# Layer 3 of a graph network: x0 times all three weights ahead of its first product, with nodes on partitions and x0's own term parked in DRAM

## The chip, the cores and the metric

The kernel runs on one core of a Trainium2 chip, in one launch. The metric is the device time in microseconds of one execution. TensorE (PE) multiplies into PSUM, VectorE (DVE) and ScalarE (ACT) move and combine results, GpSimd (POOL) and SyncE (SP) here mostly issue DMAs. All data are float32; in the trace each float32 matmul shows as two records, a transpose as one.

## The reference, cut to what matters

Four layers act on x, of 8 batches, 2048 nodes and 64 features. `A` is one 2048 x 2048 adjacency matrix, normalised by rows. Every layer ends with `x = layernorm(x + layer(x))`. The last two, the ones concerned here, are:

```python
# layer 2
out = x @ W_self + (A @ x) @ W_neigh + bias
# layer 3: support0 and support1 are both A
x1 = A @ x0;  x2 = 2 * A @ x1 - x0        # once for each support
out = concat([x0, x1, x2, x1, x2]) @ weight + bias
```

With equal supports layer 3 is three terms: `x0 (W0 - W2 - W4) + A x0 (W1 + W3) + A (A x0) (2 (W2 + W4))`, then the bias. It needs two products with A in any order of factors: `A (A x0 W_AA + x0 W_A) + x0 W_X + b`.

## The kernel before, in words

**Storage.** `xy` holds two copies of the activations in SBUF ("slots" 0 and 1), nodes on partitions: 16 tiles of 128 nodes, 512 columns (8 batches of 64 features). A "group" g is 512 nodes (4 tiles), a "pair" p is 128 columns (two batches); `part(g, p, slot)` is one 128 x 512 piece. A quarter is 1024 nodes by 256 columns, so four parts.

**A product.** `product(src, feature, ...)` computes A times slot `src` by two levels of a Strassen scheme: seven outer products A11, S1, A12, S2, S4, S3, A22, in that order, each of seven inner ones in `inner`. That makes 49 block products a product, each of a 512 x 512 piece of A (or a sum of pieces, kept in DRAM as `comb`) with a 512 x 128 operand. `load` fetches the 1 MB piece over SP's queue into a ring of 4 + 3 buffers. A block product has one of two forms:

- without `onto_slot` (line 277): four matmuls, x stationary, 512 columns of A moving. The result has features on partitions, and a "feature" function multiplies it with a weight.
- with `onto_slot` (line 270): sixteen matmuls, A stationary, 128 columns of x moving. The result has nodes on partitions, and DVE adds it straight onto the slot.

DVE forms the operand sums (t1 to t4, T) and joins the partial results (u2, u3, C); ACT copies the first partial result (p1, line 295). Three PSUM banks hold the block products and are reused by every inner product.

**Other work among the blocks.** After every block product `pump.step(rate)` lets queued generators run some steps (`jobs` first in order; `later` holds deferred ones that wake by a count of steps). So the projections, transposes and layernorms of finished parts stand between the block products in PE's instruction order. A tile framework sets the final order on each engine and the waits; it is static.

**Layers 2 and 3**, in the order of the program:

1. layer 2, `product(0, then(nothing, 1), onto_slot=1)`: slot 1 += A times slot 0, then layernorm (two pairs at a time, lines 505 to 533), which leaves x0 of layer 3 in slot 1.
2. layer 3, `product(1, feature3, own=both_terms(1, w3o, b3), rate=1.5)`: A x0 with features on partitions. For every result part `feature3` does four matmuls with W_AA (`project`, line 1161), and DVE adds them to slot 0 (line 1213). Beside it `both_terms` transposes each pair of x0 (line 1152, copied by ACT at line 1154), multiplies it with two weights (line 1190: 64 rows by 128 columns, the two batches of a pair on the two halves of the rows), and ACT and DVE bring the two results to slots 0 and 1 (lines 1195 and 1196).
3. layer 3, `product(0, then(nothing, 1, single=[(1, 0)], store=True), rate=2, onto_slot=1, ends=True)`: slot 1 += A times slot 0, layernorm, store.

PSUM beside the three banks of the products: one pool `p_z` of five banks for transposes and projections. The weights lie in `wd` (block diagonal) and `w3o`, summed and centered once early (`sum_weights`, lines 611 to 630).

Of the kernel before, what the change touches and what calls it, by code (L numbers as in the profile page):

```python
# [9 lines left out]
F32 = mybir.dt.float32  # L10
AF = mybir.ActivationFunctionType
ALU = mybir.AluOpType
AX = mybir.AxisListType
PSUM = bass.MemoryType.PSUM
DRAM = bass.MemoryType.DRAM

P = 128
EPS = 1e-5
GW = 512
TG = GW // P  # L20
# [84 lines left out]
def kernel(  # L105
# [18 lines left out]
    nc = tc.nc  # L124
# [3 lines left out]
    F = b_l0.shape[1]  # L128
    B = BF // F
    NT = N // P  # L130
    NG = N // GW
    NP = B // 2
# [5 lines left out]
    const = ctx.enter_context(tc.tile_pool(name="const", bufs=1))  # L138
# [4 lines left out]
    dram = ctx.enter_context(tc.tile_pool(name="dram", bufs=1, space=DRAM))  # L143
# [4 lines left out]
    xy = big.tile([P, 2, NT, BF], F32, tag="xy", name="xy")  # L148
# [26 lines left out]
    ident = const.tile([P, P], F32, tag="ident", name="ident")  # L175
    make_identity(nc, ident)

    W1A, W1B, W2N, W2S, W3X, W3A, W3AA = range(7)
    wd = const.tile([P, 7, P], F32, tag="wd", name="wd")

    w3o = const.tile([P, 2, F], F32, tag="w3o", name="w3o")
    w2o = const.tile([P, 2, F], F32, tag="w2o", name="w2o")
    b2 = const.tile([P, F], F32, tag="b2", name="b2")
    b3 = const.tile([P, F], F32, tag="b3", name="b3")

# [3 lines left out]
    def part(g, p, slot):  # L189
        return xy[:, slot, g * TG : (g + 1) * TG, ts(p, 2 * F)]  # L190
# [277 lines left out]
    def tiles_of(i):  # L468
        return slice(i * TG, (i + 1) * TG)

    class Norm:
# [18 lines left out]
        def center(self):  # L490
            sm = self.new("sm")
            nc.vector.tensor_reduce(sm, self.v, AX.X, ALU.add)
            nc.vector.scalar_tensor_tensor(self.v, self.wide(sm), -1.0 / F, self.v, ALU.mult, ALU.add)
# [54 lines left out]
    def layernorm(i, p0, n, slot, mean=False, store=False, pool_sq=False):  # L548

        norm = Norm(tiles_of(i), p0, n, slot, str(n), pin=False)  # L550
        if mean:
            norm.center()
        norm.square(pool_sq)
        yield
        norm.add_up()
        norm.variance()
        norm.root()
        norm.refine()
        norm.scale()
        if store:  # L560
            norm.store()
        yield

    def then(feature, slot, single=(), gap=0, after=None, **kw):


        seen = set()

        def both(i, p, hT):
            yield from feature(i, p, hT)  # L570
            seen.add((i, p))
            if (i // 2, p // 2) in single:
                yield from layernorm(i, p, 1, slot, **kw)
            elif (i, p ^ 1) in seen:
                norm = layernorm(i, p - p % 2, 2, slot, **kw)
                if gap:
                    pump.defer(norm, gap, need=i < NG // 2)
                else:
                    yield from norm
                if after is not None:  # L580
                    pump.defer(after(i, p - p % 2), 6, 2, i < NG // 2)
        return both


    if True:
# [8 lines left out]
        def load_weights():  # L594
            nc.gpsimd.memset(wd, 0.0)
            w3 = sums.tile([P, 5, F], F32, tag="t", name="w3", bufs=5)
            for k in range(2):
                half = slice(k * F, (k + 1) * F)
                for i, src in ((W1A, w_l1[0]), (W1B, w_l1[1]), (W2N, w_neigh), (W2S, w_self)):
                    nc.sync.dma_start(wd[half, i, half], src)  # L600
                nc.scalar.dma_start(w3[half], w_l3.rearrange("(k i) o -> i k o", i=F))
            nc.sync.dma_start(b2, b_l2.to_broadcast([P, F]))
            nc.sync.dma_start(b3, b_l3.to_broadcast([P, F]))
            return w3

        def sum_weights(w3):
            pin = tc.keep_in_program_order

            for k in range(2):
                half = slice(k * F, (k + 1) * F)  # L610
                pin(nc.vector.tensor_tensor(wd[half, W3A, half], w3[half, 1], w3[half, 3], ALU.add))
                pin(nc.vector.tensor_tensor(w3[half, 2], w3[half, 2], w3[half, 4], ALU.add))
                pin(nc.vector.tensor_tensor(wd[half, W3X, half], w3[half, 0], w3[half, 2], ALU.subtract))
                pin(nc.vector.tensor_scalar(wd[half, W3AA, half], w3[half, 2], 2.0, None, ALU.mult))


            for k in range(2):
                half = slice(k * F, (k + 1) * F)
                center(wd[half, W2N:, half], half, pin=pin)
            for w in (W2S, W3X):  # L620
                pin(nc.vector.tensor_tensor(wd[:, w, :], wd[:, w, :], ident, ALU.add))
            for k in range(2):
                half = slice(k * F, (k + 1) * F)
                for n, w in enumerate((W3A, W3X)):
                    pin(nc.vector.tensor_copy(w3o[half, n], wd[half, w, half]))
                for n, w in enumerate((W2N, W2S)):
                    pin(nc.vector.tensor_copy(w2o[half, n], wd[half, w, half]))
            center(b2.unsqueeze(1), pin=pin)
            center(b3.unsqueeze(1), pin=pin)

# [83 lines left out]
        with tc.tile_pool(name="p_n", bufs=4, space=PSUM) as p_n, tc.tile_pool(  # L714
            name="p_tn", bufs=2, space=PSUM
        ) as p_tn, tc.tile_pool(name="p_b", bufs=1, space=PSUM) as p_b, tc.tile_pool(
            name="xs", bufs=1
# [271 lines left out]
            for ns in range(TG):  # L989
                ch = [chunks.pop((ns, j)) for j in range(NG)]  # L990
                if ns == 0:
# [15 lines left out]
                    hT = next(first4)  # L1007
                    next(parts)
                    w3 = load_weights()
                    load_chunks(1, *AHEAD)  # L1010
                    pump.add(biases())
                else:
                    hT = fast_slice(ns, ch, held, parts if ns == 1 else ())
# [121 lines left out]
            product(1, then(feature0, 0, gap=4, pool_sq=True), lambda: pump.add(sum_wn()), rate=4, runs=RUNS)  # L1135


    late = p_z = None

    def to_late():  # L1140
        nonlocal late, p_z, p_mm2, ring2, loads
        first.close()
        late = ctx.enter_context(tc.tile_pool(name="late", bufs=1))
        ring2 = ctx.enter_context(tc.tile_pool(name="ring2", bufs=3))
        loads = 0
        p_mm2 = ctx.enter_context(tc.tile_pool(name="p_mm2", bufs=1, space=PSUM))
        p_z = ctx.enter_context(tc.tile_pool(name="p_z", bufs=5, space=PSUM))

    def pair_transposed(g, p, slot):
        pt = p_z.tile([P, GW], F32, tag="z", name="pt2")  # L1150
        for k in range(TG):
            nc.tensor.transpose(pt[:, ts(k, P)], xy[:, slot, g * TG + k, ts(p, 2 * F)], ident)  # L1152
        xT = late.tile([P, GW], F32, tag="xT", name="xT", bufs=2)
        nc.scalar.copy(xT, pt)
        return xT

    def project(terms):
        z = p_z.tile([P, TG, P], F32, tag="z", name="z")
        for k in range(TG):
            for n, (aT, w) in enumerate(terms):  # L1160
                nc.tensor.matmul(  # L1161
                    z[:, k, :], aT[:, ts(k, P)], wd[:, w, :],
                    start=(n == 0), stop=(n == len(terms) - 1),
                )
        return z
# [6 lines left out]
    def feature1b(g, p, hT):  # L1172
        z = project([(hT, W1B)])
        nc.vector.scalar_tensor_tensor(part(g, p, 0), z, 0.0, part(g, p, 0), ALU.max, ALU.add)
        yield

    product(0, feature1a, to_late, pin=True)
    def both_terms(src, w, b):

        def own(g, p):  # L1180

            xTs = [pair_transposed(g, p + q, src) for q in range(2)]
            yield

            zs = [[p_z.tile([P, TG, 2, F], F32, tag="z", name="z2") for _ in range(2)] for _ in range(2)]
            for z, xT in zip(zs, xTs):
                for k in range(TG):
                    for n in range(2):
                        half = slice(n * F, (n + 1) * F)
                        nc.tensor.matmul(z[n][:, k], xT[half, ts(k, P)], w[half], start=True, stop=True)  # L1190
            tiles = slice(g * TG, (g + 1) * TG)
            for q, z in enumerate(zs):
                for n in range(2):
                    cols = ts(2 * (p + q) + n, F)
                    nc.scalar.copy(xy[:, 0, tiles, cols], z[n][:, :, 0])
                    nc.vector.tensor_tensor(
                        xy[:, 1, tiles, cols], z[n][:, :, 1],
                        b.unsqueeze(1).to_broadcast([P, TG, F]), ALU.add,
                    )
            yield  # L1200
        return own

    def nothing(g, p, c):

        yield from ()


    product(1, then(feature1b, 0, mean=True, after=both_terms(0, w2o, b2)), rate=2)
    product(0, then(nothing, 1), onto_slot=1)


    def feature3(g, p, hT):
        nc.vector.tensor_tensor(part(g, p, 0), project([(hT, W3AA)]), part(g, p, 0), ALU.add)
        yield

    product(1, feature3, own=both_terms(1, w3o, b3), rate=1.5)
    product(0, then(nothing, 1, single=[(1, 0)], store=True), rate=2, onto_slot=1, ends=True)
    pump.drain()


# [45 lines left out]
```

## Time and profile before

| what | us |
|---|---|
| median of 3 runs | 1666.83 (1666.49 to 1666.88) |
| the profiled execution | 1666.76 |
| its span | 1665.0 |
| layer 2, second product, from the start of the span | 1092.17 to 1276.44 |
| layer 3, first product | 1276.44 to 1482.44 |
| layer 3, second product with its tail | 1482.44 to 1665.00 |

The profile is of one execution. Its time is 1.76 us longer than its span, and 0.07 us from the median. The clock granted to PE was full throughout (0.999). Busy shares are shares of the span. In the timeline the columns are start, length, engine, line, operation, output and inputs, shape, count of records; a bracket names the idle time before and what ended it. [...] the distance between starts is the cost, not the length.

### The profile page before, as it was taken

What the parts mean: (1) busy time and instruction counts of PE and PEld (TensorE: products, weight loads), DVE (VectorE), ACT (ScalarE), POOL (GpSimd) and SP (SyncE); (2) the same over time, 40 slices, a digit from 0 to 9 for tenths busy, and PEclk for the clock granted to TensorE, in tenths of its full rate; (3) what the DMA queues carried; (4) which work ended last, traced back from release to release, by engine and by line L of the source; (5) the groups of instructions that cost most, each with busy time, mean ns of one, the idle gap of its engine ahead of it and who ended that gap; (6) DMA issues with size and microseconds to landing.
All of it is one profiled execution on the core that took longest, in us unless ns stands there. A gap on an engine that the chain in (4) does not pass through costs nothing.

```text
span 1665.0 us, 21271 instructions
## 1 busy us (share of the span) xinstructions
PE 1656.7 (100%) x8414; PEld 1060.6 (64%) x8414; DVE 965.9 (58%) x1737; ACT 276.0 (17%) x810; POOL 246.1 (15%) x332
## 2 busy tenths in 40 slices
PE   9999999999999999999999999999999999999998
PEld 5988844444444444444454455599998455579998
DVE  5986895656456456655434365873668344453657
ACT  0200110242142144430010011220001011100001
POOL 1221200254155056550000000000000000000000
PEclk9999999999999999999999999999999999999999
DMA  8998899504503600019877867657888866678884
GB/s 318 340 383 310 316 322 326 200 26 162 205 26 129 250 26 26 26 65 364 290 266 278 304 254 257 229 218 272 291 297 299 306 209 233 230 264 294 316 311 167
DMA packets 81074, 391.56 MB, mean 235 GB/s; under 512 B 8944, under 2 KB 25584, under 8 KB 41040
## 3 DMA queue, kind: packets, MB, share of 16 engines
q1 hardware_dynamic: 68288, 346.78, 58.2%
q0 software_dynamic: 11248, 42.08, 6.7%
q10 hardware_dynamic: 1440, 1.35, 0.3%
q8 instruction: 67, 1.10, 0.3%
q14 instruction: 31, 0.25, 0.0%
HBM read 339.85 MB, written 50.33 MB: 234 GB/s over the span
## 4 chain that ended last, share of the span: by engine, by line
PE 95%; DVE 3%; DMA 1%; issue 0%; SPq 0%; DVEq 0%
PE y L1109 20%; PE mmb L277 17%; PE mma L277 12%; PE mmc L277 12%; PE mmb L270 9%; PE ps_n L918 7%; PE mma L270 6%; PE mmc L270 6%; PE z L1161 3%; PE z L1190 2%; PE ps_i L832 1%; DVE si L640 1%; DMA xy<-in_x 1%; PE pt L1152 1%; DMA bias<-in_b_l 0%; DVE so L640 0%
## 5 line engine op out<-in xcount | busy, mean ns | idle before, releaser
L277 PE MATMUL mmb<-a,t 128*128 128x512 f32 x648 | 292.0, 593 | 0.0
L1119 DVE SCALAR_TENSOR_TENSOR xy<-y,e_sb,xy 128x128 f32<-128x128 f32 x512 | 179.6, 351 | 141.2 <-PE y L1109 125.3
L277 PEld LDWEIGHTS mmb<-a,t 128*128 128x128 f32 x648 | 121.5, 190 | 145.3 <-issue 143.5
L1128 POOL TENSOR_TENSOR s<-s 128x512 f32<-128x512 f32 (+2 forms) x192 | 157.4, 820 | 333.0 <-ACT s L1123 322.8
L1123 ACT ACTIVATE s<-y,e_sb 128x128 f32<-128x128 f32 x512 | 139.3, 383 | 231.5 <-PE y L1109 231.5
L228 DVE TENSOR_TENSOR u<-mmb,p 128x512 f32<-128x512 f32 x84 | 57.9, 689 | 176.5 <-PE mmb L277 121.1
L270 PE MATMUL mmb<-t,a 128*128 128x128 f32 x1344 | 156.9, 275 | 0.0
L270 PEld LDWEIGHTS mmb<-t,a 128*128 128x128 f32 x1344 | 153.5, 192 | 0.0
L1109 PE MATMUL y<-wn,xT 64*128 64x512 f32 x512 | 131.5, 590 | 0.0
L1109 PE MATMUL y<-wn,C 64*128 64x512 f32 x512 | 131.2, 589 | 0.0
L1109 PE MATMUL y<-wn,tT 64*128 64x512 f32 x512 | 131.2, 589 | 0.0
L277 PE MATMUL mma<-a,T 128*128 128x512 f32 x256 | 115.5, 594 | 0.0
L277 PE MATMUL mmc<-a,t 128*128 128x512 f32 x216 | 97.3, 592 | 0.0
L295 ACT COPY p<-mma 128x512 f32<-128x512 f32 x42 | 24.7, 588 | 405.8 <-PE mma L277 248.4
L1109 PEld LDWEIGHTS y<-wn,xT 64*128 64x128 f32 x512 | 49.3, 187 | 61.2 <-issue 60.7
L1109 PEld LDWEIGHTS y<-wn,tT 64*128 64x128 f32 x512 | 49.6, 187 | 60.2 <-issue 60.2
L1109 PEld LDWEIGHTS y<-wn,C 64*128 64x128 f32 x512 | 49.5, 187 | 60.3 <-issue 60.3
L277 PE MATMUL mma<-a,xy 128*128 128x512 f32 x192 | 86.6, 594 | 0.3 <-PE pt_n L465 0.3
L277 PEld LDWEIGHTS mma<-a,T 128*128 128x128 f32 x256 | 47.6, 190 | 56.8 <-issue 56.5
L228 DVE TENSOR_TENSOR C<-mmc,C 128x512 f32<-128x512 f32 x48 | 33.2, 692 | 85.9 <-PE mmc L277 75.1
L277 PEld LDWEIGHTS mmc<-a,t 128*128 128x128 f32 x216 | 40.0, 190 | 45.4 <-issue 45.2
L277 PEld LDWEIGHTS mma<-a,xy 128*128 128x128 f32 x192 | 36.0, 190 | 44.4 <-issue 43.8
(160 smaller groups left out, 2127.5 us busy)
## 6 DMA issues: line engine op xcount, KB each, us to landing
a<-comb SPq DMA_DIRECT2D x240, 1024.0 KB, 4.8
a<-in_blocks SPq DMA_DIRECT2D x54, 1024.0 KB, 4.8
comb<-si POOLq DMA_DIRECT2D x28, 1024.0 KB, 6.2
a<-in_slices SPq DMA_DIRECT2D x15, 1024.0 KB, 9.0
comb<-so POOLq DMA_DIRECT2D x15, 512.0 KB, 9.6
t1T<-hT SPq DMA_DIRECT2D x16, 256.0 KB, 4.6
xT<-in_xT SPq DMA_DIRECT2D x16, 256.0 KB, 3.0
tT<-t1T SPq DMA_DIRECT2D x16, 256.0 KB, 3.1
```

Source lines behind the costliest of these rows:

```text
L228: nc.vector.tensor_tensor(out, a, b, op)
L270: nc.tensor.matmul(to, a[:, k, m, :], xb[:, m, :], start=(start and opens and m == 0), stop=(m == TG - 1), skip_group_check=True,)
L277: nc.tensor.matmul(ps, xb[:, m, :], a[:, :, m, :], start=(start and m == 0), stop=(m == TG - 1), skip_group_check=True,)
L295: nc.scalar.copy(p1, pa)
L640: tc.keep_in_program_order(nc.vector.tensor_tensor(out, a, b, op))
L918: nc.tensor.matmul(ps[:, ts(p, GW // 2)], b(k, p), a(k // TG, k % TG), start=(start and p == k == 0), stop=(k == NT // 2 - 1), skip_group_ ...
L1109: mm = nc.tensor.matmul(y[:, b, :], terms[n][half, ts(k, P)], wn[half, n, h * DH : (h + 1) * DH, :], start=(n == 0), stop=(n == 2),)
L1119: nc.vector.scalar_tensor_tensor(acc, y[:, :, ts(d, F)], e, acc, ALU.mult, ALU.add)
L1123: nc.scalar.activation(s[:, d], y[:, :, ts(d, F)], AF.Copy, scale=e)
L1128: nc.gpsimd.tensor_tensor(s[:, :n], s[:, :n], s[:, n : 2 * n], ALU.add)
L1161: nc.tensor.matmul(z[:, k, :], aT[:, ts(k, P)], wd[:, w, :], start=(n == 0), stop=(n == len(terms) - 1),)
L1190: nc.tensor.matmul(z[n][:, k], xT[half, ts(k, P)], w[half], start=True, stop=True)
```

## The change

Layer 3's weights are applied before the first product instead of after it. When layer 2's second product has finished and normalised two pairs, the new `three_terms` transposes x0 as before and multiplies each pair with all three weights at once (64 rows by 192 columns). Two results go by ACT into slots 0 and 1 (x0 W_AA and x0 W_A); the third, x0 W_X plus the bias, is made by DVE in `rest` and stored to DRAM (`x3`) by POOL's queue. The first product of layer 3 then runs with nodes on partitions, straight onto slot 1; meanwhile `rest_of` loads `x3` back into slot 0 where it is no longer read. The second product adds onto slot 0. `feature3` and its `project` calls are gone; `wd` shrinks to two weights.

```diff
-    product(0, then(nothing, 1), onto_slot=1)
+    product(0, then(nothing, 1, after=three_terms), to_wide, rate=1.5, onto_slot=1)
...
-    def feature3(g, p, hT):
-        nc.vector.tensor_tensor(part(g, p, 0), project([(hT, W3AA)]), part(g, p, 0), ALU.add)
+    def rest_of(g, p):
+        for q in range(2):
+            nc.gpsimd.dma_start(part(g, p + q, 0), x3[g, p + q].rearrange("p (t c) -> p t c", t=TG))
         yield
...
-    product(1, feature3, own=both_terms(1, w3o, b3), rate=1.5)
-    product(0, then(nothing, 1, single=[(1, 0)], store=True), rate=2, onto_slot=1, ends=True)
+    product(0, nothing, own=rest_of, onto_slot=1)
+    product(1, then(nothing, 0, single=[(1, 0)], store=True), to_ends, rate=2, onto_slot=0, ends=True)
```

The new function; `bufs` of the tile `xT` goes from 2 to 3, and `rest` shares that ring:

```python
    def three_terms(g, p):
        tiles = tiles_of(g)
        xT = pair_transposed(g, p, 1)
        yield
        for q in range(2):
            rest = late.tile([P, GW], F32, tag="xT", name="rest", bufs=3)
            rest4 = rest.rearrange("p (a b n f) -> p a b n f", a=2, b=2, n=2)
            zs = [p_zz.tile([P, 2, GW], F32, tag="zz", name="zz") for _ in range(2)]
            zs = [z[:, :, : 6 * F].rearrange("p a (b n f) -> p a b n f", b=2, n=3) for z in zs]
            for k in range(TG):
                for n in range(2):
                    half = slice(n * F, (n + 1) * F)
                    nc.tensor.matmul(
                        zs[n][:, k // 2, k % 2], xT[half, ts(k, P)], w3o[half], start=True, stop=True
                    )
            if q == 0:
                xT = pair_transposed(g, p + 1, 1)
            for n, z in enumerate(zs):
                cols = ts(2 * (p + q) + n, F)
                for slot in range(2):
                    to = xy[:, slot, tiles, cols].rearrange("p (a b) f -> p a b f", b=2)
                    nc.scalar.copy(to, z[:, :, :, slot])
                nc.vector.tensor_tensor(
                    rest4[:, :, :, n], z[:, :, :, 2],
                    b3.unsqueeze(1).unsqueeze(1).to_broadcast([P, 2, 2, F]), ALU.add,
                )
            nc.gpsimd.dma_start(x3[g, p + q], rest)
            yield
```

PSUM is split anew: during layer 2's second product (`to_wide`) the five banks of `p_z` become one bank for transposes and two buffers of two banks each for `zz`; at the last product (`to_ends`) two banks of `p_z` for the end. `sum_weights` does the same sums on 128 partitions in fewer instructions, and the early memset of `wd` is smaller.

More of the change, by code (lines that the diff above doesn't have):

```diff
@@ L176 @@
     make_identity(nc, ident)
-    W1A, W1B, W2N, W2S, W3X, W3A, W3AA = range(7)
-    wd = const.tile([P, 7, P], F32, tag="wd", name="wd")
-    w3o = const.tile([P, 2, F], F32, tag="w3o", name="w3o")
+    W1A, W1B = range(2)
+    wd = const.tile([P, 2, P], F32, tag="wd", name="wd")
     w2o = const.tile([P, 2, F], F32, tag="w2o", name="w2o")
+    w3o = const.tile([P, 3, F], F32, tag="w3o", name="w3o")
     b2 = const.tile([P, F], F32, tag="b2", name="b2")
@@ L598, in load_weights @@
                 half = slice(k * F, (k + 1) * F)
-                for i, src in ((W1A, w_l1[0]), (W1B, w_l1[1]), (W2N, w_neigh), (W2S, w_self)):
-                    nc.sync.dma_start(wd[half, i, half], src)
+                for to, src in (
+                    (wd[half, W1A, half], w_l1[0]), (wd[half, W1B, half], w_l1[1]),
+                    (w2o[half, 0], w_neigh), (w2o[half, 1], w_self),
+                ):
+                    nc.sync.dma_start(to, src)
                 nc.scalar.dma_start(w3[half], w_l3.rearrange("(k i) o -> i k o", i=F))
@@ L607, in sum_weights @@
             pin = tc.keep_in_program_order
+            pin(nc.vector.tensor_tensor(w3o[:, 1], w3[:, 1], w3[:, 3], ALU.add))
+            pin(nc.vector.tensor_tensor(w3[:, 2], w3[:, 2], w3[:, 4], ALU.add))
+            pin(nc.vector.tensor_tensor(w3o[:, 2], w3[:, 0], w3[:, 2], ALU.subtract))
+            pin(nc.vector.tensor_scalar(w3o[:, 0], w3[:, 2], 2.0, None, ALU.mult))
+            center(w2o, pin=pin)
+            center(w3o, pin=pin)
             for k in range(2):
                 half = slice(k * F, (k + 1) * F)
[L611 to L627, printed above, removed]
+                for w in (w2o[half, 1], w3o[half, 2]):
+                    pin(nc.vector.tensor_tensor(w, w, ident[half, half], ALU.add))
             center(b2.unsqueeze(1), pin=pin)
@@ L1135 @@
             product(1, then(feature0, 0, gap=4, pool_sq=True), lambda: pump.add(sum_wn()), rate=4, runs=RUNS)
-    late = p_z = None
+    late = p_z = p_zz = None
+    banks_z = ExitStack()
     def to_late():
@@ L1146, in to_late, with to_wide, to_ends @@
         p_mm2 = ctx.enter_context(tc.tile_pool(name="p_mm2", bufs=1, space=PSUM))
-        p_z = ctx.enter_context(tc.tile_pool(name="p_z", bufs=5, space=PSUM))
+        ctx.enter_context(banks_z)
+        p_z = banks_z.enter_context(tc.tile_pool(name="p_z", bufs=5, space=PSUM))
+    def to_wide():
+        nonlocal p_z, p_zz
+        banks_z.close()
+        p_z = banks_z.enter_context(tc.tile_pool(name="p_z1", bufs=1, space=PSUM))
+        p_zz = banks_z.enter_context(tc.tile_pool(name="p_zz", bufs=2, space=PSUM))
+    def to_ends():
+        nonlocal p_z
+        banks_z.close()
+        p_z = banks_z.enter_context(tc.tile_pool(name="p_z2", bufs=2, space=PSUM))
     def pair_transposed(g, p, slot):
@@ L1152, in pair_transposed @@
             nc.tensor.transpose(pt[:, ts(k, P)], xy[:, slot, g * TG + k, ts(p, 2 * F)], ident)
-        xT = late.tile([P, GW], F32, tag="xT", name="xT", bufs=2)
+        xT = late.tile([P, GW], F32, tag="xT", name="xT", bufs=3)
         nc.scalar.copy(xT, pt)
@@ L1205, in nothing @@
         yield from ()
+    x3 = dram.tile([NG, NP, P, TG * 2 * F], F32, tag="x3", name="x3")
+    def three_terms(g, p):
+        tiles = tiles_of(g)
+        xT = pair_transposed(g, p, 1)
+        yield
+        for q in range(2):
[3 more added lines that the diff above has]
+            zs = [z[:, :, : 6 * F].rearrange("p a (b n f) -> p a b n f", b=2, n=3) for z in zs]
+            for k in range(TG):
+                for n in range(2):
+                    half = slice(n * F, (n + 1) * F)
+                    nc.tensor.matmul(
+                        zs[n][:, k // 2, k % 2], xT[half, ts(k, P)], w3o[half], start=True, stop=True
+                    )
+            if q == 0:
+                xT = pair_transposed(g, p + 1, 1)
+            for n, z in enumerate(zs):
+                cols = ts(2 * (p + q) + n, F)
+                for slot in range(2):
+                    to = xy[:, slot, tiles, cols].rearrange("p (a b) f -> p a b f", b=2)
+                    nc.scalar.copy(to, z[:, :, :, slot])
+                nc.vector.tensor_tensor(
+                    rest4[:, :, :, n], z[:, :, :, 2],
+                    b3.unsqueeze(1).unsqueeze(1).to_broadcast([P, 2, 2, F]), ALU.add,
+                )
+            nc.gpsimd.dma_start(x3[g, p + q], rest)
+            yield
     product(1, then(feature1b, 0, mean=True, after=both_terms(0, w2o, b2)), rate=2)
-    product(0, then(nothing, 1), onto_slot=1)
-    def feature3(g, p, hT):
-        nc.vector.tensor_tensor(part(g, p, 0), project([(hT, W3AA)]), part(g, p, 0), ALU.add)
+    product(0, then(nothing, 1, after=three_terms), to_wide, rate=1.5, onto_slot=1)
+    def rest_of(g, p):
+        for q in range(2):
+            nc.gpsimd.dma_start(part(g, p + q, 0), x3[g, p + q].rearrange("p (t c) -> p t c", t=TG))
         yield
-    product(1, feature3, own=both_terms(1, w3o, b3), rate=1.5)
-    product(0, then(nothing, 1, single=[(1, 0)], store=True), rate=2, onto_slot=1, ends=True)
+    product(0, nothing, own=rest_of, onto_slot=1)
+    product(1, then(nothing, 0, single=[(1, 0)], store=True), to_ends, rate=2, onto_slot=0, ends=True)
     pump.drain()
```

## The prediction

> **What bounds the kernel now.** I read the table of busy times first, then the chain that ended last, then a table of the last three stages, and at last timelines of single stretches.
>
> ```profile
> PE 1656.7 (100%) x8414; PEld 1060.6 (64%) x8414; DVE 965.9 (58%) x1737; ACT 276.0 (17%) x810; POOL 246.1 (15%) x332
> ...
> PE 95%; DVE 3%; DMA 1%; issue 0%; SPq 0%; DVEq 0%
> ```
>
> ```profile
> 1092.17:1276.44 184.27, 184.27 (x1689) 183.54 (x1689) 113.92 (x184) 22.17 (x44) 0.00 (x0) 1.00 0.77 278
> 1276.44:1482.44 206.00, 206.00 (x835) 108.84 (x834) 94.85 (x157) 26.10 (x61) 0.00 (x0) 1.00 0.70 251
> 1482.44:1665.00 182.56, 175.99 (x1576) 175.79 (x1575) 100.19 (x180) 16.75 (x32) 0.00 (x0) 0.99 0.76 271
> ```
>
> The second fence is the table of stages: stretch, length, busy time of PE, PE's weight loads, DVE, ACT, POOL, clock, DMA share, GB/s. PE is busy for the whole of the first two stages, so the time is a sum of PE's instructions there, and any wait of PE adds to it. The prices are in the timeline of PE at the seam of the two product forms:
>
> ```profile
> 1269.13 3.74 PE L270 MATMUL mmb<-t,a 128*128 128x128 f32 x32
> 1272.71 3.74 PE L270 MATMUL mmc<-T,a 128*128 128x128 f32 x32
> 1276.28 3.60 PE L277 MATMUL mma<-a,xy 128*128 128x512 f32 x8
> 1279.71 3.60 PE L277 MATMUL mmb<-a,t 128*128 128x512 f32 x8
> ...
> 1328.65 3.60 PE L277 MATMUL mmb<-a,t 128*128 128x512 f32 x8
> 1332.18 2.06 PE L1190 MATMUL z<-w3o,xT 64*128 64x128 f32 x32
> 1334.17 1.09 PE L1152 MATMUL pt<-ident,xy 128*128 128x128 f32 x8
> 1335.10 3.60 PE L277 MATMUL mma<-a,xy 128*128 128x512 f32 x8
> ...
> 1344.15 1.05 PE L1161 MATMUL z<-wd,C 128*128 128x128 f32 x8
> 1345.04 3.60 PE L277 MATMUL mmc<-a,t 128*128 128x512 f32 x8
> ```
>
> From start to start: a block with nodes on partitions 3.573 us, with features on partitions 3.433; eight transposes 0.87; one `feature3` 0.89; one call of line 1190 1.99, with its edges 2.17 (1328.65 to 1335.10 is 6.45, less 3.43 and 0.87, some 2.15; where a block follows directly, that block is 0.1 longer).
>
> [...] 64-row records of 512 columns come every 215 ns (82.60 us for 384 in the chain), full ones every 429. [...] line 1196 of DVE waited 6.4 us in all for line 1195 of ACT, which reads the same tile. [...] 3.3 us for `out` on SP's queue, 9.8 for 256 KB of `comb` on POOL's, early, beside heavier traffic.
>
> **The change part by part, on PE.**
> - `feature3` goes: 16 calls of 0.89, -14.2 us (one of them ran at the start of the last stage).
> - 49 blocks change form: 49 x (3.573 - 3.433) = +6.8.
> - 128 matmuls grow from 128 to 192 columns. From 429 ns at 512 and 111.6 at 128 a column costs 0.83 ns, a record 5.5 besides. Two row halves side by side: at least (192 x 0.83 + 5.5)/2 = 82 ns a record; at most the 62 measured plus 64 x 0.83/2, 88.5. A step of `three_terms` has 16 records, 1.32 to 1.42 us, and 0.19 for its edges; 16 steps 24.2 to 25.7, middle 25.0, in place of 8 x 2.17 = 17.4: +7.6 (6.8 to 8.3).
> - Transposes: 64 before and after, 0.
>
> The sum is +0.2 us (-0.6 to +0.9): by count alone the change is nothing.
>
> **Costed at nothing**, with the cover: the 16 stores and 16 loads of x3, 4.2 MB each way, the loads in 512-byte packets. The last stage already carries its 17 stores of `out` in such packets beside the same 3.57 us a block, DMA share 0.76, no wait of PE; a ring of seven pieces covers six blocks, 21 us against 4.8 to landing. POOL has no other work there (0.00 busy); its loads wait for readers of slot 0, and stores queued behind them are due later by the static order. The weights' sums are at 94 to 99 us with PE full; the smaller memset is at 0.9 us, ahead of DMAs that the chain waits for. Were a cover gone, each is under 1 us. DVE loses 16 adds of line 1213 (11 us) and all in all gains work in a product with nodes on partitions (114 against 95 us a stage); below 65%, no bound by its sum, but its order matters.
>
> **The new wait.** A step fills both `zz` buffers, so the next step's matmuls wait until ACT (four copies of 0.33) and, after it, DVE (two adds of 0.35) have emptied them. Before, five banks made that free. In the static order of the changed kernel most steps have a whole block and a transpose between them, 4.0 us, enough. Two places do not.
>
> *Pairs finished by S4* (in layer 2's A22). PE's order: transpose, block, step, transpose, 5/16 block, transpose, 11/16 block, step, transpose, 2/16 block, step. DVE's: up to the next reduction the same operations as now, here in the timeline of before:
>
> ```profile
> 1251.47 0.69 DVE L228 TENSOR_TENSOR C<-mmc,C 128x512 f32<-128x512 f32 x1 [0.95 <-PE mmc L270]
> ...
> 1257.02 1.22 DVE L533 TENSOR_TENSOR xy<-xy,rs 128x1024 f32<-128x1024 f32 x1
> 1258.15 0.69 DVE L228 TENSOR_TENSOR C<-xy,C 128x512 f32<-128x512 f32 x1
> 1258.75 0.68 DVE L228 TENSOR_TENSOR u<-mmb,p 128x512 f32<-128x512 f32 x1
> ```
>
> S3's last block ended at 1251.27; counted from it, DVE is free at 7.5. Then come the reduction 1.15, two adds for the first step (9.35), variance, reciprocal, ACT's root and three small ones (10.7), scaling 1.13 (11.85), four of `inner`'s own 2.55 (14.4), and only then the adds of the second step: 14.75 and 15.1. PE wants the third step at 0.44 + 3.57 + 1.5 + 0.44 + 1.12 + 0.44 + 2.45 + 1.5 + 0.44 + 0.45 = 12.35. It waits some 2.8 us. Behind it on PE stand fourteen matmuls of a block, and everything after: [...]
>
> *Pairs finished by S3* (in layer 3's first A11). The same order, a whole block more between the first two steps. The one transpose bank is emptied after four copies: 0.4 us at the third transpose. Then only 0.9 us stand between the second and third step, while ACT needs 1.3 and DVE 0.35 more: 0.8 us. Together 1.2.
>
> So 4.0 us of waits. The trace of before has no such wait; bounds are 0 (DVE arrives in time) and, with the next item, some 14.
>
> *Stores that must land.* `rest` shares three buffers with `xT`: the second step's adds above need the first step's store (ready at 9.4) landed by 14.4, so 5.0 us for issue and landing. I take that it just fits: `out`'s 3.3 and POOL's 0.65 to issue. At 9.8 it would add 4.8 here, 3.4 where the third transposed pair after A12 needs a buffer, 1.5 after S3.
>
> The sum on the profiled execution: 1666.76 + 0.2 + 4.0 = 1671.0; the median stands 0.07 above it, no difference. About 0.2% (3.3 us) is what a measurement of this kernel can tell from no change.
>
> **Rivals.**
> 1. *The waits are covered, the count decides.* It decides if DVE reaches the second step's adds at 12.3, not 15.1, which takes 2.8 us out of its queue; the gaps between its operations here are 0 to 1.1, so a little is possible. Then 1667.0 with half a us of wait, range 1665 to 1669: no change. Against it: the durations are measured, and the order is static.
> 2. *Stores land late and DVE or ACT is held with all behind it.* For it: POOL's 9.8 us. Against: that was at a DMA share near 1. 1674 to 1681.
> 3. *A faster kernel.* It takes matmuls of 192 columns at no more than the 62 ns of 128, 16 x 16 x 23 ns = 5.9 less, and no wait: 1661. For it: at 128 columns something other than columns may set the pace (62 against 56 by columns). Against it: columns alone ask for 82.
>
> That the change doesn't do what it says: the static order shows the form changed, `feature3` gone and 16 steps of eight 192-column matmuls.
>
> **How the numbers follow.** Forecast 0.52 (1669 to 1673.5), rival 2 0.18, rival 1 0.20, rival 3 0.10. Slower: all of rival 2 and most of the forecast, 0.62; faster: rival 3 and a little, 0.11; the same 0.27. The range leaves out rival 3 and the slow end of rival 2: 1665.0 to 1679.0.
>
> **What would show it.** Step by step: layer 3's first product near 3.57 us a block; the steps at 1.3 to 1.4 us; PE idle on DVE at the third step of the S4 pairs, near 3 us, and less at the S3 pairs; no wait of PE for DMA. I am wrong if PE shows no idle time there, if the stores hold DVE, or if the steps take under 1.1 us.

## The result and the profile after

The changed kernel takes 1671.38 us (median of 7 runs, 1671.19 to 1672.98) against 1666.83 before (7 runs, 1666.27 to 1667.00): 1.003 times as long, 95% interval 1.002 to 1.0041. It is slower, by 4.5 us or 0.3%. Below, "after" is the profiled execution of the changed kernel: 1671.23 us, span 1669.5, which is 4.5 more than the span before.

The table of busy times, and the chain that ended last by engine:

```profile
PE 1659.1 (99%) x9462; PEld 1153.9 (69%) x9462; DVE 966.2 (58%) x1727; ACT 284.5 (17%) x842; POOL 265.9 (16%) x364
...
PE 23%; DVE 0%; ACT 0%; issue 0%; DVEq 0%
```

PE is still the bound: its busy time grew by 2.4 us, and its idle time (span less busy time) by 2.1. The chain, which ran through 95% of the span on PE before, now covers only a quarter: followed back from the end it breaks off at 1273.89, at a wait of PE. Ask the trace what PE waited for in its matmuls of `zz` and that place is named; the columns are microseconds in all, times, and the longest:

```profile
PE zz L1235 <- DVE rest L1245: 1.8, 2, 1.7
```

The stages, cut at the starts of the two products (columns as in the prediction's table):

```profile
1091.50:1295.42 203.92, 202.17 (x1855) 198.42 (x1854) 120.00 (x204) 36.66 (x85) 5.14 (x9) 1.00 0.74 262
1295.42:1487.97 192.55, 192.32 (x1726) 189.30 (x1725) 91.95 (x139) 20.26 (x51) 15.64 (x23) 1.00 0.84 300
1487.97:1669.50 181.53, 175.26 (x1570) 175.06 (x1568) 99.80 (x180) 16.75 (x32) 0.00 (x0) 0.99 0.78 274
```

Layer 2's second product took in the new steps and grew by 19.65 us, with 1.75 us in which PE is idle. Layer 3's first product shrank by 13.45, although each of its blocks now takes longer. Together +6.2. The last stage is 1.03 shorter, mostly because one `feature3` (0.89) no longer runs into it, and everything ahead of layer 2's second product is 0.67 shorter by the marks of the two tables, 0.51 by the starts of the block itself (1092.01 and 1091.50). The sum is the 4.5 us of the span.

PE's timeline, first at the pairs finished by A12, then at those finished by S4, at last at those finished by S3:

```profile
1204.75 3.74 PE L271 MATMUL mmb<-t,a 128*128 128x128 f32 x32
1208.41 1.57 PE L1235 MATMUL zz<-w3o,xT 64*128 64x192 f32 x16
1209.91 0.66 PE L1163 MATMUL pt<-ident,xy 128*128 128x128 f32 x4
1210.41 3.74 PE L271 MATMUL mma<-xy,a 128*128 128x128 f32 x32
...
1259.16 0.60 PE L1163 MATMUL pt<-ident,xy 128*128 128x128 f32 x4
...
1269.65 1.57 PE L1235 MATMUL zz<-w3o,xT 64*128 64x192 f32 x16
1271.15 0.66 PE L1163 MATMUL pt<-ident,xy 128*128 128x128 f32 x4
1271.64 0.61 PE L271 MATMUL mma<-T,a 128*128 128x128 f32 x4
1273.94 1.90 PE L1235 MATMUL zz<-w3o,xT 64*128 64x192 f32 x16 [1.68 <-DVE rest L1245]
1275.76 3.39 PE L271 MATMUL mma<-T,a 128*128 128x128 f32 x28
...
1309.04 1.57 PE L1235 MATMUL zz<-w3o,xT 64*128 64x192 f32 x16
...
1311.81 2.12 PE L1235 MATMUL zz<-w3o,xT 64*128 64x192 f32 x16 [0.16 <-DVE rest L1245]
```

In the first four lines nothing waits, so they give the price of a step: 5.66 us from block to block, less 3.573 for the block (its records last 3.74, but the next block starts 3.573 after it) and 0.435 for four transposes, is 1.65; where two blocks enclose it without transposes (1278.99 to 1287.83) it is 1.69. In the third step at S4 PE stood for 1.68 us before it, and the step itself takes 0.32 longer than one that waits for nothing (1.90 against 1.57 in length). At S3 the idle time before the step is small, but the step is 0.54 longer: the records of the second buffer waited inside the group, where no bracket shows it. They begin 0.55 us after those of the first, just behind VectorE's second addition, which ends at 1312.30. The length of a group of matmuls has to be read beside the bracket.

### The profile page after: what moved, and what is told of

Read it like the earlier page. It is cut to its first block, busy times and chain, and to the rows that moved or that the text cites. A ratio compares the mean times of both kernels' runs of the same rounds, so it can differ in the third digit from the quotient of the medians.

```text
span 1669.5 us, 23512 instructions
## 1 busy us (share of the span) xinstructions
PE 1659.1 (99%) x9462; PEld 1153.9 (69%) x9462; DVE 966.2 (58%) x1727; ACT 284.5 (17%) x842; POOL 265.9 (16%) x364
## 3 DMA queue, kind: packets, MB, share of 16 engines
q0 software_dynamic: 13808, 50.47, 8.0%
q10 hardware_dynamic: 1440, 1.35, 0.2%
## 5 line engine op out<-in xcount | busy, mean ns | idle before, releaser
L271 PE MATMUL mmb<-t,a 128*128 128x128 f32 x2016 | 236.0, 275 | 0.0
L271 PEld LDWEIGHTS mmb<-t,a 128*128 128x128 f32 x2016 | 230.4, 192 | 0.2 <-issue 0.2
L278 PE MATMUL mmb<-a,t 128*128 128x512 f32 x480 | 215.8, 592 | 0.0
L278 PEld LDWEIGHTS mmb<-a,t 128*128 128x128 f32 x480 | 90.4, 190 | 109.5 <-issue 108.5
L271 PE MATMUL mma<-T,a 128*128 128x128 f32 x768 | 90.0, 275 | 0.0
L271 PEld LDWEIGHTS mma<-T,a 128*128 128x128 f32 x768 | 87.8, 192 | 0.3 <-issue 0.2
L278 PE MATMUL mma<-a,T 128*128 128x512 f32 x192 | 86.5, 593 | 0.0
L271 PE MATMUL mmc<-t,a 128*128 128x128 f32 x672 | 78.7, 275 | 0.0
L271 PEld LDWEIGHTS mmc<-t,a 128*128 128x128 f32 x672 | 76.7, 192 | 0.4 <-issue 0.4
L278 PE MATMUL mmc<-a,t 128*128 128x512 f32 x160 | 72.1, 592 | 0.0
```

What stands on the lines that cost most here:

```text
L271: nc.tensor.matmul(to, a[:, k, m, :], xb[:, m, :], start=(start and opens and m == 0), stop=(m == TG - 1), skip_group_check=True,)
L278: nc.tensor.matmul(ps, xb[:, m, :], a[:, :, m, :], start=(start and m == 0), stop=(m == TG - 1), skip_group_check=True,)
```

## The experiments

Each edit is against the changed kernel (e) or the kernel before (b). What the changed kernel costs was open in two terms: waits of PE for a free `zz`, and PE's own count. The rivals were late stores, and a cost of the early weights. The second needs no experiment: layer 2's second product starts between 1091.38 and 1092.08 in the six profiles with the new weights and between 1091.52 and 1092.01 in the four with the old ones, so the traces show neither a cost nor a gain of them.

**e1: one tick more between the steps.** `defer` wakes `three_terms` every third tick instead of every second (a tick is one step of the queue, and 1.5 of them are taken at each block here), so that a whole block stands between all steps of the pairs.

```diff
-                    pump.defer(after(i, p - p % 2), 6, 2, i < NG // 2)
+                    pump.defer(after(i, p - p % 2), 6, 2 if slot == 0 else 3, i < NG // 2)
```

> The changed kernel with one number changed: deferred steps of three_terms wake every 3 ticks, not every 2, so that in PE's static order every step has at least a whole block product (3.57 us) or more before the next. Same instructions otherwise. Theory (PE waits for the two zz buffers at the S4 and S3 pairs, 3.3 us in the trace): PE shows no idle time there and the time falls by 2.5 to 3.5 us, to 1668 to 1669, still above the kernel before by about 1.5. Rival D (the traffic of x3 is what costs): the time stays within 0.7 us of 1671.4.

Measured: 1667.89 us (13 runs, 1667.65 to 1668.02); 1.0007 times before, interval 0.9999 to 1.0015. The median stands 1.35 us above the 1666.54 of the runs of before beside it, but the interval doesn't tell the two apart. Its table of stages, cut at the same instructions, and its timeline at the S4 pairs:

```profile
1091.60:1293.19 201.59, 201.59 (x1855) 198.10 (x1854) 120.05 (x204) 36.63 (x85) 5.16 (x9) 1.00 0.74 264
```

```profile
1267.41 1.57 PE L1235 MATMUL zz<-w3o,xT 64*128 64x192 f32 x16
1268.91 0.66 PE L1163 MATMUL pt<-ident,xy 128*128 128x128 f32 x4
1269.40 3.74 PE L271 MATMUL mma<-T,a 128*128 128x128 f32 x32
1273.07 1.57 PE L1235 MATMUL zz<-w3o,xT 64*128 64x192 f32 x16
```

PE is busy for all of the 201.59 us, no step has a bracket, and each is 1.57 long. The same instructions (x1855 in both) take 2.33 us less than in after; layer 3's first product takes 191.53 (1293.19 to 1484.72), 1.02 less. The waits are therefore worth 3.3 us in the profile and 3.5 in the medians. What is left, with no wait at all, is the count: the two stages together are 393.12 against 390.27 before, +2.85, of which 0.89 is the `feature3` that left the last stage: +1.96.

**e2: two ticks more.** `else 4` in the same line.

> The same with 4 ticks. Now the close steps stand at the pairs finished by A12 and by A22, and those of S4 and S3 are a block or more apart. Theory: the waits follow the closeness of steps, so they leave S4 and S3 and show at A12 and A22; DVE has no layernorm there, so ACT's four copies and DVE's two adds alone bound them, about 0.8 us at the third step and 0.2 at a transpose in each place, 2 us in all; time 1669.5 to 1671. Rival (the waits belong to what DVE does in S4's stretch, whatever the steps do): waits stay at S4.

Measured: 1671.2 us in one run, 0.2 above the expected range. The waits followed the closeness of the steps: S4 and S3 are free of them, but the static order has moved: now the A12 pairs have a step with little ahead of it.

```profile
1228.09 0.61 PE L271 MATMUL mmc<-xy,a 128*128 128x128 f32 x4
1229.63 1.97 PE L1235 MATMUL zz<-w3o,xT 64*128 64x192 f32 x16 [0.93 <-DVE rest L1245]
```

Four records of a block (2/16) stand between two steps, the same pattern as at S4 in after; the pairs of layer 2's A22 have it as well, with the numbers of after's S3 (0.16 before, 2.12 long). Layer 2's second product (1092.08 to 1295.36) takes 203.28 us, 1.69 more than in e1, and layer 3's first (to 1487.92) 192.56, 1.03 more. With the 0.48 by which it starts later, which no edit explains, that is the 3.2 us between the two spans (1669.4 and 1666.2). So spacing by ticks isn't monotonic: what counts is what the order puts between two steps.

**e3: without the trip to DRAM.** Neither the 16 stores nor the 16 loads; x0 W_X is missing from the result.

```diff
-            nc.gpsimd.dma_start(x3[g, p + q], rest)
...
-    product(0, nothing, own=rest_of, onto_slot=1)
+    product(0, nothing, onto_slot=1)
```

> The changed kernel without the 16 stores to x3 and the 16 loads from it: leaves out x0's own term and the bias at the end (slot 0 keeps x0 W_AA). DVE still makes rest. The instruction order on PE is the same. Theory: the transfers are covered, time within 1 us of the changed kernel's 1671.4, waits at the third steps as in it. Rival D: 2 us or more less.

Measured: 1672.83 us (6 runs, 1671.36 to 1673.56), 1.0033 times before (1.0021 to 1.0045): no faster than after, so the 8.4 MB cost nothing, and the late stores fall as a cause. The expectation, within 1 us of after, was missed: the median is 1.45 above. PE's timeline shows the same wait in the same place (the line numbers are one lower here), and something new behind it; the third fence is the table of two windows.

```profile
1274.36 2.71 PE L1234 MATMUL zz<-w3o,xT 64*128 64x192 f32 x16 [1.69 <-DVE rest L1244]
1277.01 4.19 PE L271 MATMUL mma<-T,a 128*128 128x128 f32 x28
```

```profile
1274.00:1278.00 4.00, 3.64 (x20) 3.20 (x21) 1.27 (x4) 1.27 (x4) 0.00 (x0) 0.66 0.05 20
1278.00:1282.00 4.00, 4.00 (x35) 4.00 (x34) 0.91 (x2) 0.00 (x0) 0.00 (x0) 0.91 0.00 0
```

The wait is as long as after's, but the step takes 2.71 us against 1.90 and the block's remainder 4.19 against 3.39. The eighth column of the windows says why: the granted clock is 0.66 and 0.91 here, where after's profile has 1.00 in both. From the step's start to that of the next block there are 6.67 us here and 5.05 in after: 1.6 us lost to the clock, after a wait of 1.69. Three of after's seven runs lie 1.2 to 1.8 us above the other four, and four of the six here lie over 1 us above the other two; none of e1's thirteen does, where PE doesn't wait. The mean clock of each run fits: it is 0.998 in these seven upper runs and 0.999 in the six lower ones, and 0.001 of 1670 us is 1.7 us. So my estimate, from this profile and these means, is that the upper runs of after are executions with such a stretch of lower clock, and that e3's higher median is four of them in six; its two lower runs, 1671.36 and 1671.67, stand beside after's lower four. For after itself no profile shows it: its profiled run is one of the lower four. Nor is it the only cause of spread: of the 19 runs of before beside these, four stand 1.2 to 1.9 us above the lowest, at a mean clock of 0.999, and the profile of before has no such wait.

**e4: two terms of three.** The matmuls have 128 columns in place of 192; the term x0 W_X is left out (`rest` is made from x0 W_A in its place).

```diff
-                        zs[n][:, k // 2, k % 2], xT[half, ts(k, P)], w3o[half], start=True, stop=True
+                        zs[n][:, k // 2, k % 2], xT[half, ts(k, P)], w3o[half, :2], start=True, stop=True
```

> The changed kernel with two weights instead of three in each step: matmuls of 128 columns, and DVE makes rest from the second result (leaves out x0 W_X). Everything else stays: 16 steps of 16 records, the same copies and adds. It prices a step. If a record costs what the columns ask (0.83 ns a column, halved for two row halves) and a step has a fixed 0.2 us inside it whatever its length, a step falls from 1.50 to about 1.09 us. If a step has no fixed part (62 ns a record as in the kernel before), 0.99. If a record of 192 columns costs more than its columns ask (94 ns), the fall is the larger. Time: 16 x 0.41 = 6.5 less than the changed kernel, near 1665, waits of PE at S4 much as before since DVE sets them.

Measured: 1664.27 us in one run, 7.0 less than after's profile.

```profile
1204.63 3.74 PE L271 MATMUL mmb<-t,a 128*128 128x128 f32 x32
1208.29 1.16 PE L1235 MATMUL zz<-w3o,xT 64*128 64x128 f32 x16
1209.38 0.66 PE L1163 MATMUL pt<-ident,xy 128*128 128x128 f32 x4
1209.88 3.74 PE L271 MATMUL mma<-xy,a 128*128 128x128 f32 x32
...
1270.98 2.09 PE L1235 MATMUL zz<-w3o,xT 64*128 64x128 f32 x16 [1.13 <-DVE rest L1245]
```

The same stretch as in after takes 5.25 us against 5.66: 0.41 a step, 25.6 ns for 64 columns in each of 16 records, which is 6.5 us over 16 steps. The wait at S4 (the last line) is no shorter, it only stands elsewhere: 1.13 before the step and 0.93 inside it (2.09 in length against 1.16), 2.06 together, where after has 1.68 and 0.32. So 192 columns do cost by their columns, and the third rival falls. This stretch says more: the distance from the step's start to the next is 1.094 for 16 records and was 1.985 for 32 before, of the same shape. Twice the records are 0.89 us more, 55.7 ns each, so that 0.20 us of a group does not depend on its size. The single records of before's own group at 1338.63 show where it lies: they start in pairs, the two row halves 0.007 us apart, and the pairs follow each other after 0.112 us, but the second follows the first after 0.214, and the next block the last pair after 0.208. Twice as many groups pay it twice as often.

**b1, b2, b3: the parts of the count on the kernel before.** b1 leaves out `feature3` (A A x0 W_AA is missing); b2 also gives that product the form with nodes on partitions; b3 changes only the rate at which layer 2's second product takes in other work.

```diff
-    product(1, feature3, own=both_terms(1, w3o, b3), rate=1.5)
+    product(1, nothing, own=both_terms(1, w3o, b3), rate=1.5)                  # b1
+    product(1, nothing, own=both_terms(1, w3o, b3), rate=1.5, onto_slot=0)     # b2
...
-    product(0, then(nothing, 1), onto_slot=1)
+    product(0, then(nothing, 1), rate=1.5, onto_slot=1)                        # b3
```

> The kernel before with feature3 left out (leaves out the whole term A A x0: its 16 projections and the adds to slot 0), the first product of layer 3 still with features on partitions. Theory: every PE instruction of it is on the path, 16 x 0.89 = 14.2 us less: 1652.6. A rival in which the projections are partly hidden gives less than that, 1655 or more.

> As the last one, and the first product of layer 3 has its results with nodes on partitions, straight onto slot 0 (leaves out the weight of that term). Theory: the form alone costs 49 x (3.573 - 3.433) = 6.8 us over the last one: 1659.4. Rival: the added DVE adds onto the slot or the more numerous weight loads make it dearer, 1662 or more, or the form costs nothing, 1653.

> The kernel before with rate=1.5 in layer 2's second product, as the changed kernel has it. Theory: no difference beyond 0.7 us of 1666.8, the layernorms only stand elsewhere. Rival: bunching them holds up PE, 1668 or more.

Measured, one run each: 1652.39, 1659.48 and 1666.56 us. Against the median before, `feature3` is worth 14.4, and the other form of 49 blocks costs 7.1 (b2 less b1). The rate alone does nothing (-0.3). The one run of before beside these took 1667.68, so the stages in the traces are the better witness. In b1 layer 3's first product takes 192.60 us (1276.20 to 1468.80), 13.40 less than before, and the rest 0.90 less: 14.3 in all. In b2 the product takes 200.11 (1275.79 to 1475.90), 7.5 more than in b1, of which 0.25 is idle time of PE; its earlier start hides 0.4 of that in the whole time. In b3 it takes 206.05, against 206.00 before.

**e5: who empties the buffers late?** ScalarE's copies and VectorE's additions both have to be done before a `zz` is free. Here the additions read SBUF, so the copies alone count (x0 W_X is missing from the result).

```diff
-                    rest4[:, :, :, n], z[:, :, :, 2],
+                    rest4[:, :, :, n], b3.unsqueeze(1).unsqueeze(1).to_broadcast([P, 2, 2, F]),
```

> This kernel leaves out the term x0 W_X: VectorE's two additions of a step read a buffer in SBUF in place of zz, so that ScalarE's four copies alone have to be done before a zz buffer is used again; TensorE's count of matmuls is that of after. If VectorE's long queue behind the transposes' work sets the wait at S4 (1.76 us before the third step and 0.32 inside), what is left there is ScalarE's own lateness, as at S3: 0.5 to 1.0 us, the time comes to 1669.5 to 1670.5, and the runs that stand 1.5 us above the rest are fewer or gone. If the closeness of three steps alone sets it, whoever empties the buffers, the third step waits 1.7 us again and the time stays at 1671 or above. In this kernel the third step of S4 stands directly after the transposes, which gives ScalarE some 0.6 us less time; that works against the first reading.

Measured: 1670.22 us (10 runs, 1669.87 to 1670.86), 1.0021 times before (1.0012 to 1.0031); 1.2 less than after, and no run stands 1.5 above the rest. PE's timeline at S4, and DVE's beside it:

```profile
1271.19 0.66 PE L1163 MATMUL pt<-ident,xy 128*128 128x128 f32 x4
1271.99 2.12 PE L1235 MATMUL zz<-w3o,xT 64*128 64x192 f32 x16
1274.03 3.84 PE L271 MATMUL mma<-T,a 128*128 128x128 f32 x32
```

```profile
1270.97 0.69 DVE L229 TENSOR_TENSOR u<-mmb,p 128x512 f32<-128x512 f32 x1
1271.58 0.75 DVE L1245 TENSOR_TENSOR rest<-b 128x256 f32<-128x256 f32 x2
...
1275.42 1.43 DVE L1245 TENSOR_TENSOR rest<-b 128x256 f32<-128x256 f32 x4 [1.29 <-DMA x<-rest]
```

The third step now starts 0.80 us after the transposes' start, where a transpose followed by other work takes 0.5, and is 0.55 longer than a free one: some 0.9 us of waiting are left. They are ScalarE's own. At S3 nothing is gained: layer 3's first product takes 192.55 us (1294.13 to 1486.68), the same as in after. There the second addition of after ends 0.46 us behind ScalarE's last copy (1312.30 and 1311.84), and in e5 the step comes 0.45 earlier in the order, which takes that back. From the first transpose of S4 (1259.19) to the next product's first block (1294.13) it takes 34.94 us; in after 36.26. VectorE's queue therefore sets at least 1.3 of the 2.3 us at S4 (the step comes 0.45 earlier in the order here too, which favours the wait), and the closeness of three steps over two buffers the rest. The last DVE line shows what is late next: with the additions moved forward, they wait 1.29 us for a store of `rest` to land, and since nobody waits for them any more, PE doesn't notice.

## Why the prediction was right, and where its sizes were off

The forecast of 1671.0 had the sign, the mechanism and its two places; the profiled execution took 1671.23. By its own steps:

- *`feature3` goes, -14.2.* b1: -14.4, or -14.3 by its stages, and -0.90 of it shows up in the last stage, as the text had it.
- *49 blocks in the other form, +6.8.* b2 less b1: +7.1, or +7.5 by the stage. Blocks stand 3.57 us apart in the changed product, which is 6.9 for 49, so the price was right; what b2 has beyond that and its 0.25 of idle time was not traced.
- *Sixteen steps at 1.51 to 1.61 us with their edges.* This term was mis-sized. A step takes 1.65 to 1.69, so 16 of them 26.7, not 25.0. The price per column was right (25.6 ns for 64 against 26.5 taken); what was missing is that the 62 ns of a record before was a mean over a group of 32 and held a fixed 0.20 us per group. A group of 16 costs 1.09 at 128 columns, not half of 1.985. PE's count is then +1.9 instead of +0.2, which e1 shows without any wait (+1.96). A step takes 1.50 between its edges, above the 1.3 to 1.4 that the prediction named as a sign.
- *Wait at S4, 2.8.* Measured 2.3: 1.68 before the step, 0.32 inside it, and 0.24 ahead of the second transposes, whose one bank ACT empties at 1266.55; the prediction had that last wait at S3 alone. DVE's timeline of after, from the reduction on:

```profile
1266.64 1.21 DVE L513 TENSOR_REDUCE ss<-sq 128x16 f32<-128x1024 f32 x1
1267.77 0.75 DVE L1245 TENSOR_TENSOR rest<-zz,b 128x256 f32<-128x256 f32 x2
...
1269.79 1.22 DVE L534 TENSOR_TENSOR xy<-xy,rs 128x1024 f32<-128x1024 f32 x1
...
1272.86 0.69 DVE L229 TENSOR_TENSOR C<-xy,C 128x512 f32<-128x512 f32 x1
1273.46 0.75 DVE L1245 TENSOR_TENSOR rest<-zz,b 128x256 f32<-128x256 f32 x2
```

  It is the order that the prediction wrote down, to within 0.05 us: counted from S3's last block (1259.16) the last two additions end at 14.7 and 15.05 (0.42 and 0.75 after 1273.46), predicted 14.75 and 15.1. That DVE would take its list in this order was the author's assumption; the records here start in that order, from 1266.64 to 1273.46. PE came later than predicted, at 12.9 by the starts of its records (13.1 by the end of the last one, from which the bracket counts) instead of 12.35: the two steps ahead of it were 0.35 longer with their edges, and the transposes waited 0.24. And it starts when the first of the two buffers is free, not the second: at 1273.94, with the two additions ending at 1273.88 and 1274.21. The mis-sized step so took part of its cost back from the wait.
- *Wait at S3, 1.2.* Measured 1.0.
- *Stores land within 5.0 us.* The trace of after says of the tile `rest`:

```profile
DMA to landing us min/median/max: 2.3/2.6/6.0
```

  The median is 2.6 us, nearer to the 3.3 of `out` than to the 9.8 of the early stage, which was the wrong neighbour; the longest took 6.0. The store that S4's second additions needed was issued at 1268.81 and had landed at 1271.14, more than 2 us ahead of them. e3 shows that stores and loads cost PE nothing, so rival 2 is out. The loads did not go in packets of 512 bytes, which would be 8192 of them: POOL's queue has 2560 packets more than before for stores and loads together (13808 and 11248), with 8.39 MB more.
- *Edits costed at nothing.* The start of layer 2's second product is 0.51 earlier and the tail 0.30 shorter. Neither was foreseen. The start is scatter as far as the profiles tell (the starts named ahead of e1). The tail stays open: from the last product's first block to the end of the span after takes 181.48 us, but e3, without the trip to DRAM, takes 181.77, and so does the kernel before without `feature3` (181.78 in b1 and b2).

The sum in the trace: 1.96 of count, 3.35 of waits, less 0.81 at the two ends is the 4.5 measured. The forecast had 0.2 and 4.0. The sign and the places were earned; that the total comes within 0.3 us is luck, because three deviations of 0.7 to 1.7 us (count, waits and ends) nearly cancel.

The spread of the runs, up to 1.8 us above the lowest, was not in the forecast.

No version here beats both kernels. e1 is the best of the complete ones: its median is 1.35 us above the time before, which its interval doesn't tell from no change. Without waits the trade is 14.2 us of projections for 6.9 of the other form and 9.3 of longer steps.

## What to carry to other kernels

When a stage is bound by PE's instruction order, sum the change by counts, but price a smaller group of matmuls from a group of its own size: half a group cost more than half here (1.094 us for 16 records, 1.985 for 32). Where the PSUM buffers of a step shrink to two, write out the queue of the engine that empties them, in its order, up to the moment PE comes back; that gave the wait at S4 to half a microsecond from a trace that did not contain it. If such a wait is found, look first for a place in the order with a whole block between the steps: one tick more bought back 3.5 of the 4.5 us here, and two lost most of them again.

## What the runs showed of the hardware

- A group of matmuls of 64 rows (two row halves in turn, float32) has a fixed part: 1.985 us for 32 records of 128 columns (before), 1.094 for 16 (e4), so 55.7 ns a record and 0.20 us a group. Half of it lies behind the first pair of records (0.214 us to the second, where later pairs take 0.112) and half behind the last (0.208). Another 0.15 to 0.19 comes where the group borders on full-height blocks (1.65 to 1.69 a step in after, of which 1.50 lies between its edges).
- In one profile the granted clock fell after a short wait. In e3 a PE idle time of 1.69 us is followed by 0.66 of the clock from 1274 to 1278 and 0.91 from 1278 to 1282, 1.6 us lost; before and behind that, from the start of the span to 1490, it is 1.00. In after's profile 1.68 us idle was followed by full clock, 1.00 in both stretches, and in stretches of 4 us the traces of before and after have 1.00 throughout up to 1660. So an idle time of this length was followed by the lower clock in one profile of two. What decides in which executions was not tried.
